# A graph layer on one core: the vector engine's transform steps placed by estimated times, row norms a stage earlier, the last transform step done pair by pair, one load moved to another queue

## The chip, the core and the metric

The kernel runs on one core of a Trainium2 chip, in fp32 throughout. A core has a matrix engine (TensorE, PE in the rows of the profile; PEld is its weight load), a vector engine (VectorE, DVE), a scalar engine (ScalarE, ACT), GpSimd (POOL) and SyncE (SP). Each engine works through its own instructions in order and waits on semaphores for the others. Transfers are issued from the instruction streams of SP, ACT or POOL, in the order of that stream, and then run on 16 DMA engines which all streams share. Matmul results land in PSUM, everything else lives in SBUF.

The metric is device time in microseconds, the median of several runs. Before the change: 2670.3 us, the median of 3 runs from 2668.56 to 2674.92.

## The reference

`x` is 64 graphs of 256 nodes with 256 features, `adj` 64 matrices of 256 x 256 zeros and ones. Cut to what matters:

```
h      = relu(layernorm(x))                       # per node
c      = relu(bn1(conv1(h)))                      # 1 tap, 256 -> 256 channels
x_conv = relu(bn2(conv2(c)) + h)                  # 17 taps along the nodes
s      = h @ w_se.T + b_se                        # 3 numbers per node
A      = exp(-dist2(s, s)) * adj
x_nmp  = A @ relu(h @ w_msg.T + b_msg)
gi, gh = [x_conv, x_nmp] @ w_ih.T, h @ w_hh.T     # three gates r, z, n of 256 each
n      = tanh(gi_n + sigmoid(gi_r + gh_r) * gh_n)
out    = x + (1 - z) * n + z * h                  # z = sigmoid(gi_z + gh_z)
```

## The kernel before

**Tiling.** Two graphs make a pair (tiles of 128 partitions x 512 columns), four pairs a block; there are 32 pairs and 8 blocks. In the code `i` is a pair, `b` a block, `j` a pair within the block. Work that needs one pair is called per pair: `norm` (layer norm: statistics on VectorE, a power on GpSimd, the scaling on VectorE), `transpose_h` (TensorE transposes, relu on ScalarE, result `hT`), `conv1`, `split`, `embed` (s), `message`, `affinity` (exp on ScalarE, then a product with `adj` on VectorE), `transpose_a`, `aggregate` (x_nmp, tile `xnm`), `gates` (called twice per pair, for the two halves of the channels) and `finish` (transposes back, adds x from tile `y`, stores).

**The convolution in transform space.** The 17-tap convolution is done for a whole block at once, as a short Fourier transform over 16 phases of the nodes, products of 16 frequency bins with the transformed filter, and a transform back. The transforms run on VectorE as lists of elementwise steps. `split` writes sums and differences of neighbouring positions into the tiles U and V. `fft.odd` (on V, temporary T, result also in Sv) gives the operands of bins 0 to 7, `fft.even` (on U, with PT and T) those of bins 8 to 15. `products(b, m)` does bins 2m and 2m+1: 24 matmul groups into three PSUM tiles, then a ScalarE copy and two VectorE instructions that read them out into Yv (m under 4) or Yu (m from 4 on; Yu is the tile V, used again). The way back is `odd_back` on Yv, `q_back` and `p_back` on Yu, `join` (four instructions that put the two halves together in V and Yv) and `residual` (adds `hT`, relu on ScalarE). The `gates` of a pair read its part of Yv.

**What sets the order.** Every engine's order is the order in which the Python code calls its instructions: nothing is rescheduled later. The transform steps are held in a queue; `pump(us)` takes steps off it until their estimated time is used up, at places chosen by hand, and `drain()` empties it. Before `gates(i, 0)` the queue is drained, all four pairs are joined and `residual` runs for all four. Inside that call, between the products that read `hT` and `xnm` and those that read Yv, the function `more` calls `conv1` of the next block's first pair.

**Buffers.** PSUM has five tiles `acc` and three tiles `aux`, taken in turn. `wb` holds three frequency bins of the filter, 768 KB each, loaded from a DRAM copy (`filt`): `products(b, m)` issues the load of bin 2m+2 ahead of its matmuls and that of bin 2m+3 behind them, each into the buffer of the bin used three before. `x` has two buffers, `adj` one, `y` one, `h1` (the result of conv1) one. SP issues the loads of `wb`, `x` and `adj`, POOL those of `y` and the stores.

A list of lines of the profile: L59, L62, L65 and L69 are the transform's steps (multiply-add, add, subtract, scaling on ScalarE), L474 to L482 `norm`, L491 `transpose_h`, L498/L500 `conv1`, L511/L512 `split`, L522 the load of a bin, L547 the products, L562/L563 their reading out, L579/L580 `residual`, L586 to L590 `embed`, L599/L602 `message`, L611 to L617 `affinity`, L627 `transpose_a`, L637 `aggregate`, L652 the products of `gates` with L658 to L682 behind them, L690 to L692 `finish`, L303 the loads of x, adj and y.

Of the kernel before, what the change touches and what calls it, by code (L numbers as in the profile page):

```python
# [38 lines left out]
class Fft:  # L39
# [27 lines left out]
    def scale(self, x, s):  # L67
        def run():
            self.a.mul(x, x, s)  # L69
            return 0  # L70
        return run
# [73 lines left out]
    def odd_back(self, Y, T):  # L145

        q = []
# [28 lines left out]
        for s in (0, 4):  # L176
            q += [self.scale(Y(0, s + 1), C8),
                  self.scale(Y(1, s), C16),
                  self.scale(Y(1, s + 1), C16 * C8),
                  self.scale(Y(0, s + 2), R2),  # L180
                  self.scale(Y(0, s + 3), R2 * C8),
                  self.scale(Y(1, s + 2), R2 * C16),
                  self.scale(Y(1, s + 3), R2 * C16 * C8)]
        return q

    def q_back(self, Y, T):

        q = [self.sub(T(0, 0, 4), Y(0, 0, 4), Y(1, 0, 4)),
# [11 lines left out]
        for s in (0, 2):  # L200
            q += [self.scale(Y(0, s + 1), R2), self.scale(Y(1, s), C8), self.scale(Y(1, s + 1), R2 * C8)]
        return q
# [28 lines left out]
def kernel(  # L231
# [155 lines left out]
    for k in range(DC):  # L387
# [9 lines left out]
        for s in fft.odd(V, T, Sv):  # L397
            s()
# [6 lines left out]
        for s in fft.even(U, PT, T):  # L405
            s()
# [49 lines left out]


    queue = deque()

    def pump(us):  # L460
        while queue and us > 0:
            us -= queue.popleft()() / 960.0 + 0.1

    def drain():
        pump(1e9)
# [4 lines left out]
    def norm(i):  # L470
        st = work.tile([P, G * MC, 6], FP, name="st")
        mv = work.tile([P, G * MC, 2], FP, name="mv")
        for j in range(G * MC):
            nc.vector.bn_stats(st[:, j, :], X[i][:, j, :])  # L474
# [170 lines left out]
    def gates(i, dc, middle=None):  # L645
# [17 lines left out]
        if middle:  # L663
            middle()
# [178 lines left out]
```

## Time and profile before

| what | value |
|---|---|
| median of 3 runs | 2670.3 us |
| the profiled execution, its own time | 2674.03 us |
| its span from first to last instruction | 2672.3 us |
| mean granted TensorE clock (1 is full) | 0.899 |
| PE busy | 2026.6 us, 76% of the span |
| DVE busy | 1485.3 us, 56% |
| ACT busy / POOL busy | 635.4 us / 127.6 us |
| DMA | 186.91 MB, mean 70 GB/s |

One profiled execution gives all rows. In a row of the timeline stand start, duration, engine, line, operation, output and inputs, the count that was merged (a fp32 matmul counts as two passes), and in brackets the idle time ahead of it and what ended it. A duration of matmuls contains a modelled end, so lengths of PE work are taken from start to start. In a row of the waits stand who waited for whom, the sum, the number and the longest. A row of the stretches gives the busy time of each engine between two times, then the granted clock, the share of the DMA engines and GB/s.

The first 217 us load and transform the filter and prepare the first block. After that the profile repeats per block, 310 to 315 us each for the first seven; the last block, which prepares no next one, takes 271 us.

### The profile page before, as it was taken

The numbers are of one execution on the slowest core, as the hardware profiler recorded it, in microseconds if no ns is written. First come the engines' busy times: TensorE is split into PE (matmuls) and PEld (weight loads), VectorE is DVE, ScalarE is ACT, GpSimd is POOL, SyncE is SP. The second block draws the span as 40 slices with busy tenths as digits, with TensorE's granted clock in tenths as the row PEclk, the third lists the DMA queues.
The fourth block names the chain that finished last, engine by engine and source line by source line (L and its number), as shares of the span: only waits on it lengthen the run. The fifth ranks groups of instructions, "written<-read, shape, count | busy, mean of one in ns | idle before, by whom it ended". The sixth has DMA issues, their size and how long they took to land.

```text
span 2672.3 us, 20737 instructions
## 1 busy us (share of the span) xinstructions
PE 2026.6 (76%) x7744; PEld 1266.3 (47%) x7744; DVE 1485.3 (56%) x2641; ACT 635.4 (24%) x1077; POOL 127.6 (5%) x191
## 2 busy tenths in 40 slices
PE   0035878886897778968788868986789777888698
PEld 0015634474445644456344744456444563447454
DVE  6846743568346663467435683367634674356822
ACT  0011322123221132113221232211321132212321
POOL 1010000000000000000000000000000000000000
PEclk9977889988999789988899879998899888998899
DMA  5433201141022401142012410214011420114101
GB/s 144 144 107 103 96 15 48 40 149 67 17 59 56 165 16 36 39 134 87 24 33 50 154 67 11 65 52 158 28 32 44 122 99 24 36 32 154 36 16 40
DMA packets 73941, 186.91 MB, mean 70 GB/s; under 512 B 15184, under 2 KB 32080, under 8 KB 73840
## 3 DMA queue, kind: packets, MB, share of 16 engines
q1 hardware_dynamic: 49152, 144.98, 16.5%
q0 software_dynamic: 18992, 33.78, 5.6%
q10 hardware_dynamic: 5696, 6.82, 0.8%
q8 instruction: 61, 1.00, 0.2%
q14 instruction: 40, 0.33, 0.0%
HBM read 156.39 MB, written 29.10 MB: 69 GB/s over the span
## 4 chain that ended last, share of the span: by engine, by line
PE 62%; DVE 19%; issue 5%; DMA 5%; ACT 4%; POOL 1%; SPq 1%; DVEq 0%; POOLq 0%; ACTq 0%
PE acc L652 33%; PE acc L547 12%; PE acc L498 5%; DMA wb<-filt 5%; PE aux L599 4%; PE aux L637 2%; PE aux L491 2%; DVE T L62 2%; DVE e L617 2%; DVE V L59 2%; DVE Yv L65 2%; PE aux L586 2%; DVE T L65 1%; ACT Yv L580 1%; DVE V L65 1%
## 5 line engine op out<-in xcount | busy, mean ns | idle before, releaser
L652 PE MATMUL acc<-hT,w_hh 128*128 128x512 f32 x768 | 350.6, 592 | 0.0
L652 PE MATMUL acc<-xnm,w_ih 128*128 128x512 f32 x768 | 350.5, 592 | 0.0
L652 PE MATMUL acc<-Yv,w_ih 128*128 128x512 f32 x768 | 342.6, 596 | 8.7 <-ACT Yv L580 8.7
L668 DVE SCALAR_TENSOR_TENSOR gn<-tr,gn 128x512 f32<-128x512 f32 x64 | 44.3, 692 | 513.2 <-ACT tr L667 513.2
L491 PE MATMUL aux<-ident,x 128*128 128x128 f32 x256 | 62.3, 392 | 244.3 <-DVE x L482 210.1
L652 PEld LDWEIGHTS acc<-Yv,w_ih 128*128 128x128 f32 x768 | 146.5, 192 | 190.3 <-issue 180.9
L498 PE MATMUL acc<-hT,w_c 128*128 128x512 f32 x256 | 162.3, 785 | 93.4 <-ACT gn L658 93.4
L652 PEld LDWEIGHTS acc<-xnm,w_ih 128*128 128x128 f32 x768 | 145.9, 190 | 183.7 <-issue 183.7
L652 PEld LDWEIGHTS acc<-hT,w_hh 128*128 128x128 f32 x768 | 144.1, 190 | 161.6 <-issue 158.4
L547 PE MATMUL acc<-U,wb 128*128 128x128 f32 x1024 | 145.0, 305 | 89.4 <-DMA wb<-filt 66.5
L547 PE MATMUL acc<-Sv,wb 128*128 128x128 f32 x512 | 84.0, 317 | 163.7 <-issue 68.9
L547 PEld LDWEIGHTS acc<-U,wb 128*128 128x128 f32 x1024 | 140.0, 219 | 95.4 <-DMA wb<-filt 68.4
L667 ACT ACTIVATE tr<-acc,b_rz 128x512 f32<-128x512 f32 x64 | 44.0, 687 | 549.9 <-PE acc L652 549.9
L491 PEld LDWEIGHTS aux<-ident,x 128*128 128x128 f32 x256 | 42.2, 187 | 264.2 <-DVE x L482 168.0
L511 DVE TENSOR_TENSOR V<-h 128x512 f32<-128x512 f32 x64 | 44.1, 689 | 217.2 <-ACT h L500 217.2
L547 PEld LDWEIGHTS acc<-Sv,wb 128*128 128x128 f32 x512 | 76.6, 227 | 172.5 <-issue 74.5
L59 DVE SCALAR_TENSOR_TENSOR V<-T,V 128x256 f32<-128x256 f32 (+2 forms) x280 | 152.7, 609 | 0.2
L547 PE MATMUL acc<-V,wb 128*128 128x128 f32 x1024 | 145.4, 303 | 0.0
L498 PEld LDWEIGHTS acc<-hT,w_c 128*128 128x128 f32 x256 | 61.8, 256 | 172.7 <-ACT gn L658 99.2
L547 PEld LDWEIGHTS acc<-V,wb 128*128 128x128 f32 x1024 | 141.4, 221 | 0.0
L599 PE MATMUL aux<-w_msg,hT 128*128 128x256 f32 x512 | 121.0, 391 | 19.8 <-ACT hT L492 19.8
L599 PEld LDWEIGHTS aux<-w_msg,hT 128*128 128x128 f32 x512 | 100.0, 197 | 52.0 <-ACT hT L492 25.9
(133 smaller groups left out, 2714.5 us busy)
## 6 DMA issues: line engine op xcount, KB each, us to landing
wb<-filt SPq DMA_DIRECT2D x120, 768.0 KB
x<-in_x_dram SPq DMA_DIRECT2D x64, 256.0 KB
adj<-in_adj_dram SPq DMA_DIRECT2D x64, 256.0 KB
y<-in_x_dram POOLq DMA_DIRECT2D x64, 256.0 KB, 5.7
out_dram<-y POOLq DMA_DIRECT2D x64, 256.0 KB, 5.2
V<-in_c_wT_dram ACTq DMA_DIRECT2D x32, 128.0 KB
filt<-V SPq DMA_DIRECT2D x8, 512.0 KB
wb<-filt SPq DMA_DIRECT2D x8, 512.0 KB
```

What stands on the lines that cost most here:

```text
L59: return self.step(out, lambda: self.v.scalar_tensor_tensor(out, x, s, y, op0=ALU.mult, op1=ALU.add))
L62: return self.step(out, lambda: self.v.tensor_add(out, x, y))
L65: return self.step(out, lambda: self.v.tensor_sub(out, x, y))
L491: nc.tensor.transpose(chunk(p, j // MC, j % MC), X[i][:, j, dc * P:(dc + 1) * P], ident)
L498: nc.tensor.matmul(p, w_c1[:, k, o * P:(o + 1) * P], HT[i][:, k, :], start=(k == 0), stop=(k == DC - 1))
L547: nc.tensor.matmul(p[kind][:, (n * DC + o) * P:(n * DC + o + 1) * P], WB[b, 2 * m + n][:, kind, k, o * P:(o + 1) * P], v[:, k::DC, 0, :], ...
L586: nc.tensor.matmul(p[:KD, :], w_se[:, k, :], HT[i][:, k, :], start=(k == 0), stop=(k == DC - 1))
L599: nc.tensor.matmul(p[:, c * D:(c + 1) * D], chunk(HT[i][:, k], g, c), w_msg[:, k, :], start=(k == 0), stop=(k == DC - 1))
L617: nc.vector.tensor_mul(e, e, ADJ[i][:, g * MC + c].rearrange("p (b h c) -> p c h b", c=MC, b=NW))
L637: nc.tensor.matmul(graph(p, g), MSG[i][:, g, c, dc * P:(dc + 1) * P], AT[i][:, g, c, :], start=(c == 0), stop=(c == MC - 1))
L652: nc.tensor.matmul(p, w[:, row:row + P], r, start=first and j == 0, stop=last and j == len(terms) - 1)
L668: nc.vector.scalar_tensor_tensor(gn, tr, 1.0, gn, op0=ALU.add, op1=ALU.mult)
```

## The change

The `pump` calls go. A class `Pace` keeps an estimate of how far TensorE and VectorE are: matmuls add their columns times 0.431/512 us per pass, VectorE instructions their elements over 960 plus 0.1 us. Ahead of a VectorE instruction that waits for another engine, `pace.vector` takes steps off the queue as long as the next one, by the estimate, ends by the time at which that input is ready; `flush(mark)` takes all steps up to a mark, where their result is needed. Other parts of the change:

- `odd` and `even` of the next block are queued behind its last `split`; what is left of `odd` is flushed ahead of `products(b, 0)`, what is left of `even` ahead of `products(b, 4)`.
- `embed` and `message` of a block's first pair come ahead of `products(b, 0)`.
- `join` is cut by pair (`part`) into four times four instructions, each four followed by that pair's `residual`; before `gates(i, 0)` reads Yv only pair 0 is flushed.
- `conv1` of the next block's first pair comes ahead of `affinity(i + 2)`, out of the middle of `gates`. `norm` of the pairs behind it is called a stage before their `transpose_h`; `x` loads are called right behind `transpose_h`.
- `adj` is loaded from POOL's stream, `y` has two buffers and is loaded two pairs ahead.
- The ScalarE scalings of `odd_back` and `q_back` become half as many instructions of twice the size, called between steps of the next part.

The core of the diff:

```diff
-        def run():
-            call()
-            return n
-        return run
+        return n, call
...
+    def odd_factors(self, Y):
+        return [self.scale(Y(c, s, 2, 4), f) for c, s, f in (
+            (0, 1, C8), (1, 0, C16), (1, 1, C16 * C8), (0, 2, R2), (0, 3, R2 * C8), (1, 2, R2 * C16),
+            (1, 3, R2 * C16 * C8))]
...
-    def join(self, Yu, Yv, T):
-        return [self.add(T(None, 0, 4), Yu(None, 4, 4), Yu(None, 0, 4)),
-                self.sub(Yu(None, 4, 4), Yu(None, 4, 4), Yu(None, 0, 4)),
-                self.sub(Yv(None, 0, 4), T(None, 0, 4), Yv(None, 0, 4)),
-                self.sub(Yv(None, 4, 4), Yu(None, 4, 4), Yv(None, 4, 4))]
+    def join(self, Yu, Yv, T, part):
+        yu, yv, t = (lambda s, v=v: v(None, s, 4).rearrange("p (o g) n e -> p o g (n e)", o=2)[:, :, part]
+                     for v in (Yu, Yv, T))
+        return [self.add(t(0), yu(4), yu(0)),
+                self.sub(yu(4), yu(4), yu(0)),
+                self.sub(yv(0), t(0), yv(0)),
+                self.sub(yv(4), yu(4), yv(4))]
+class Pace:
+    def __init__(self):
+        self.pe = self.dve = 0.0
+        self.queue = deque()
+    def tensor(self, columns):
+        self.pe += columns * 2 * 0.431 / 512
+    def run(self):
+        n, call = self.queue.popleft()
+        call()
+        if n:
+            self.dve += n / 960.0 + 0.1
+    def vector(self, n, ready=0.0):
+        while self.queue and self.dve + self.queue[0][0] / 960.0 <= ready:
+            self.run()
+        self.dve = max(self.dve, ready) + (n / 960.0 + 0.1 if n else 0.0)
+    def add(self, steps, mark=None):
+        self.queue.extend(steps)
+        if mark:
+            self.queue.append((0, mark))
+            mark.left = True
+    def flush(self, mark):
+        while mark.left:
+            self.run()
+        self.sync()
+    def sync(self):
+        self.pe = max(self.pe, self.dve + 0.2)
+class Mark:
+    left = False
+    def __call__(self):
+        self.left = False
...
-        load_rows(ADJ[i], adj, i, nc.sync)
+        load_rows(ADJ[i], adj, i, nc.gpsimd)
     def load_y(i):
-        Y[i] = work.tile([P, G * MC, D], FP, name="y")
+        Y[i] = work.tile([P, G * MC, D], FP, name="y", bufs=2)
...
+    pace = Pace()
+    def mm(p, w, v, columns, **kw):
+        nc.tensor.matmul(p, w, v, **kw)
+        pace.tensor(columns)
+    def transpose(p, v):
+        nc.tensor.transpose(p, v, ident)
+        pace.tensor(P / 2)
+    PSUM, ACT = 0.2, 0.9
...
         nc.gpsimd.tensor_tensor(rstd, rstd, neg_half, ALU.pow)
-        pump(1.2)
+        pace.vector(0, pace.dve + 1.4)
...
+        if i + 2 < B // G:
+            load_x(i + 2)
...
+        pace.vector(0, pace.pe + ACT)
...
+            pace.vector(2 * W, pace.pe + PSUM)
             nc.vector.tensor_sub(re, pv[0], pv[2])
             nc.vector.tensor_add(im, pv[0], pv[1])
...
-        if middle:
-            middle()
+        if wait:
+            wait()
         product(pr, xc, r, False, True)
         tr = work.tile([P, W], FP, name="tr")
         nc.scalar.activation(tr, pr, AF.Tanh, bias=b_rz[:, dc:dc + 1], scale=0.5)
+        pace.vector(W, pace.pe + ACT)
         nc.vector.scalar_tensor_tensor(gn, tr, 1.0, gn, op0=ALU.add, op1=ALU.mult)
-        pump(1.5)
         product(pn, xc, n, False, True)
+        pace.vector(W, pace.pe + PSUM)
...
-        if i + 1 < B // G:
-            load_y(i + 1)
-    def prepare(b, j, stats=True):
-        if b < NB:
-            i = b * PB + j
-            if stats:
-                norm(i)
-            transpose_h(i)
-            conv1(i)
-            split(j)
-            if i + 2 < B // G:
-                load_x(i + 2)
+        if i + 2 < B // G:
+            load_y(i + 2)
+    def mix(a, b):
+        q, done = [], 0
+        for j, step in enumerate(a):
+            q.append(step)
+            while done < (j + 1) * len(b) // len(a):
+                q.append(b[done])
+                done += 1
+        return q
+    odd, even, q_done = Mark(), Mark(), Mark()
+    joined = [Mark() for _ in range(PB)]
+    def forward():
+        pace.add(fft.odd(V, T, Sv), odd)
+        pace.add(fft.even(U, PT, T), even)
     load_bin(0, 0)
     load_bin(0, 1)
     load_y(0)
+    load_y(1)
     for j in range(PB):
-        prepare(0, j)
+        norm(j)
+        transpose_h(j)
+        conv1(j)
+        split(j)
+    forward()
     for b in range(NB):
         i = b * PB
-        if b == 0:
-            queue.extend(fft.odd(V, T, Sv))
-            drain()
-            queue.extend(fft.even(U, PT, T))
-        products(b, 0)
-        pump(4)
+        nxt = i + PB
         embed(i)
         message(i)
-        products(b, 1)
-        pump(5)
+        pace.flush(odd)
+        products(b, 0)
         affinity(i)
         if b > 0:
             finish(i - 1)
+        products(b, 1)
+        transpose_a(i)
         products(b, 2)
-        pump(6)
-        transpose_a(i)
+        aggregate(i)
         products(b, 3)
-        drain()
-        queue.extend(fft.odd_back(Yv, T))
-        aggregate(i)
+        pace.flush(even)
+        pace.add(fft.odd_back(Yv, T))
+        embed(i + 1)
         products(b, 4)
-        pump(6)
-        embed(i + 1)
         message(i + 1)
         products(b, 5)
-        pump(5)
+        pace.add(mix(fft.q_back(Yu, T), fft.odd_factors(Yv)))
         affinity(i + 1)
-        queue.extend(fft.q_back(Yu, T))
+        norm(nxt)
         products(b, 6)
-        pump(8)
-        if b + 1 < NB:
-            norm(i + PB)
         transpose_a(i + 1)
         products(b, 7)
-        queue.extend(fft.p_back(Yu, T))
-        queue.extend(fft.join(Yu, Yv, T))
+        pace.add(mix(fft.p_back(Yu, T), fft.q_factors(Yu)))
+        for j in range(PB):
+            pace.add(fft.join(Yu, Yv, T, slice(2 * G * j, 2 * G * (j + 1))))
+            pace.add([(W, lambda i=i, j=j, o=o: residual(i + j, o)) for o in range(DC)], joined[j])
         aggregate(i + 1)
-        pump(8)
-        if b + 1 < NB:
-            transpose_h(i + PB)
+        transpose_h(nxt)
         embed(i + 2)
         message(i + 2)
-        pump(5)
+        conv1(nxt)
         affinity(i + 2)
-        drain()
-        for j in range(PB):
-            residual(i + j)
-        def more(b=b, i=i):
-            if b + 1 < NB:
-                conv1(i + PB)
-                split(0)
-                if i + PB + 2 < B // G:
-                    load_x(i + PB + 2)
-            transpose_a(i + 2)
-        gates(i, 0, more)
+        def wait(j=0):
+            pace.flush(joined[j])
+        gates(i, 0, wait)
+        pace.flush(joined[1])
+        split(nxt)
+        norm(nxt + 1)
         gates(i, 1)
+        transpose_a(i + 2)
+        transpose_h(nxt + 1)
         aggregate(i + 2)
-        prepare(b + 1, 1)
+        conv1(nxt + 1)
+        pace.flush(joined[3])
+        split(nxt + 1)
+        norm(nxt + 2)
         gates(i + 1, 0)
         embed(i + 3)
+        transpose_h(nxt + 2)
         message(i + 3)
-        prepare(b + 1, 2)
+        conv1(nxt + 2)
+        split(nxt + 2)
         finish(i)
+        norm(nxt + 3)
         gates(i + 1, 1)
         affinity(i + 3)
         gates(i + 2, 0)
+        transpose_h(nxt + 3)
         transpose_a(i + 3)
-        prepare(b + 1, 3)
+        conv1(nxt + 3)
+        split(nxt + 3)
         if b + 1 < NB:
-            queue.extend(fft.odd(V, T, Sv))
-            even = fft.even(U, PT, T)
-            queue.extend(even)
+            forward()
         finish(i + 1)
         gates(i + 2, 1)
         aggregate(i + 3)
         gates(i + 3, 0)
         finish(i + 2)
         gates(i + 3, 1)
-        while b + 1 < NB and len(queue) > len(even):
-            queue.popleft()()
     finish(B // G - 1)```

Three places in the order of the instructions, as it stands in the two programs.

SP, one block of the stream. Before (`adj` is the load of a pair's adjacency, `wb` that of one bin):

```order
L522 DMA wb<-filt 128x1536 x4
L303 DMA adj<-in_adj_dram 128x1x512 x2
L522 DMA wb<-filt 128x1536 x8
L303 DMA adj<-in_adj_dram 128x1x512 x2
L522 DMA wb<-filt 128x1536
L522 DMA wb<-filt 128x1024
```

Now:

```order
L580 DMA wb<-filt 128x1536 x2
L343 DMA x<-in_x_dram 128x1x512 x8
L580 DMA wb<-filt 128x1536 x13
L580 DMA wb<-filt 128x1024
L580 DMA wb<-filt 128x1536 x2
```

The loads of `adj` between those of the bins have gone from this stream (they stand in POOL's), and the x loads of a block stand together.

PE, from the transposes of the next block's first x to the first products that read Yv. Before:

```order
L491 MATMUL aux<-ident,x 128x128 x8
L586 MATMUL aux<-hT,w_se 67x512 x2
L599 MATMUL aux<-w_msg,hT 128x256 x8
L611 MATMUL aux<-rd,ld 128x256 x4
L652 MATMUL acc<-hT,w_hh 128x512 x4
L652 MATMUL acc<-xnm,w_ih 128x512 x4
L652 MATMUL acc<-hT,w_hh 128x512 x2
L652 MATMUL acc<-xnm,w_ih 128x512 x2
L498 MATMUL acc<-hT,w_c_105 128x512 x4
L627 MATMUL aux<-ident,e 128x128 x8
L652 MATMUL acc<-Yv,w_ih 128x512 x6
```

Now (all matmuls of helpers bear the line of `mm`, L500, and of `transpose`, L504):

```order
L504 MATMUL aux<-ident,x 128x128 x8
L500 MATMUL aux<-hT,w_se 67x512 x2
L500 MATMUL aux<-w_msg,hT 128x256 x8
L500 MATMUL acc<-hT,w_c_105 128x512 x4
L500 MATMUL aux<-rd,ld 128x256 x4
L500 MATMUL acc<-hT,w_hh 128x512 x4
L500 MATMUL acc<-xnm,w_ih 128x512 x4
L500 MATMUL acc<-hT,w_hh 128x512 x2
L500 MATMUL acc<-xnm,w_ih 128x512 x2
L500 MATMUL acc<-Yv,w_ih 128x512 x6
```

`conv1` (w_c) has moved ahead of `affinity` (rd, ld), and `transpose_a` (ident, e) behind the gates.

DVE, from the end of `p_back` to the first instructions of `gates(i, 0)`. Before:

```order
L65 TENSOR_TENSOR V<-T,V 128x16x32
L62 TENSOR_TENSOR T<-V 128x2048
L65 TENSOR_TENSOR V<-V 128x32x64
L65 TENSOR_TENSOR Yv<-T,Yv 128x32x64
L65 TENSOR_TENSOR Yv<-V,Yv 128x32x64
L579 SCALAR_TENSOR_TENSOR Yv<-Yv,bn_scale,hT 128x512 x8
L511 TENSOR_TENSOR V<-h_398 128x8x64
L512 TENSOR_TENSOR U<-h_398 128x8x64
L511 TENSOR_TENSOR V<-h_398 128x8x64
L512 TENSOR_TENSOR U<-h_398 128x8x64
L668 SCALAR_TENSOR_TENSOR gn<-tr,gn 128x512
```

Now:

```order
L58 TENSOR_TENSOR T<-V 128x2x256
L61 TENSOR_TENSOR V<-V 128x2x4x64
L61 TENSOR_TENSOR Yv<-T,Yv 128x2x4x64
L61 TENSOR_TENSOR Yv<-V,Yv 128x2x4x64
L638 SCALAR_TENSOR_TENSOR Yv<-Yv,bn_scale,hT 128x512 x2
L58 TENSOR_TENSOR T<-V 128x2x256
L61 TENSOR_TENSOR V<-V 128x2x4x64
L61 TENSOR_TENSOR Yv<-T,Yv 128x2x4x64
L61 TENSOR_TENSOR Yv<-V,Yv 128x2x4x64
L728 SCALAR_TENSOR_TENSOR gn<-tr,gn 128x512
L731 SCALAR_TENSOR_TENSOR gn<-gn,acc 128x512
L638 SCALAR_TENSOR_TENSOR Yv<-Yv,bn_scale,hT 128x512
```

The four big instructions of `join` and the eight of `residual` are now four small and two for pair 0, then the next pair's ahead of and among the gates' own; `split` (h) follows later.

More of the change, by code (lines that the diff above doesn't have):

```diff
@@ L396 @@
         nc.vector.tensor_sub(V(0, 4), V(0, 4), e0)
-        for s in fft.odd(V, T, Sv):
-            s()
+        for _, step in fft.odd(V, T, Sv):
+            step()
         for c in range(2):
@@ L404 @@
             put(c * 4, 1, k, V(c, 0, 4)[:, 0])
-        for s in fft.even(U, PT, T):
-            s()
+        for _, step in fft.even(U, PT, T):
+            step()
         for c in range(2):
@@ L651, in product @@
             for j, (w, r) in enumerate(terms):
-                nc.tensor.matmul(p, w[:, row:row + P], r, start=first and j == 0, stop=last and j == len(terms) - 1)
+                mm(p, w[:, row:row + P], r, W, start=first and j == 0, stop=last and j == len(terms) - 1)
         r, z, n = dc * P, D + dc * P, 2 * D + dc * P
```

92 lines of the change are left out of this document (45 added, 47 removed).

## The prediction

> **What bounds the kernel now.** The page first, then the granted clock by stretches, then who waited for whom on TensorE (PE) in one whole block, then that block's timeline.
>
> ```profile
> PE 2026.6 (76%) x7744; PEld 1266.3 (47%) x7744; DVE 1485.3 (56%) x2641; ACT 635.4 (24%) x1077; POOL 127.6 (5%) x191
> 1405.00:1452.00 47.00, 47.00 (x128) 23.02 (x127) 26.78 (x38) 7.55 (x12) 3.65 (x6) 1.00 0.19 44
> 1230.00:1238.90 8.90, 0.00 (x0) 0.00 (x0) 8.90 (x24) 0.48 (x1) 0.00 (x0) 0.56 0.82 261
> ```
>
> No engine is full over the span. Where PE isn't held up (second row, between gates) it works 47.00 of 47 us at clock 1.00; where it waits (third row) the clock is 0.56 while DVE is full. So the limit is PE's own work plus waits that other engines or loads set. The block from 1151.94 to 1466.25 us (314.3 us) has these:
>
> ```profile
> PE acc L547 <- DMA wb<-filt: 17.2, 2, 9.1
> PE acc L498 <- ACT gn L658: 13.3, 1, 13.3
> PE acc L547 <- issue: 9.8, 1, 9.8
> PE aux L491 <- DVE x L482: 6.8, 2, 4.4
> PE aux L491 <- issue: 4.9, 1, 4.9
> PE acc L547 <- DVE U L62: 2.9, 1, 2.9
> PE aux L599 <- ACT hT L492: 2.8, 1, 2.8
> ```
>
> With 1.7 in four smaller ones they sum to 59.4 us ("issue" names no releaser: the 9.8 ends when DVE's last step of `odd` is done, the 4.9 when x is normalised). Behind each of the nine larger waits PE starts slowly. Two of them from the timeline:
>
> ```profile
> 1188.19 2.07 PE L547 MATMUL acc<-Sv,wb 128*128 128x128 f32 x8 [8.07 <-DMA wb<-filt]
> 1193.47 1.08 PE L547 MATMUL acc<-Sv,wb 128*128 128x128 f32 x8
> 1202.66 7.25 PE L547 MATMUL acc<-U,wb 128*128 128x128 f32 x48 [2.87 <-DVE U L62]
> 1209.75 1.88 PE L586 MATMUL aux<-hT,w_se 128*67 128x512 f32 x4
> 1211.47 3.62 PE L599 MATMUL aux<-w_msg,hT 128*128 128x256 f32 x16
> 1214.92 5.52 PE L547 MATMUL acc<-U,wb 128*128 128x128 f32 x48
> 1220.28 1.89 PE L611 MATMUL aux<-rd,ld 67*128 67x256 f32 x8
> 1222.01 1.06 PE L547 MATMUL acc<-U,wb 128*128 128x128 f32 x8
> ```
>
> Two bins take 5.36 us warm (1214.92 to 1220.28), one 2.68. Behind the wait of 8.07 one takes 5.28 (2.6 lost), behind that of 2.87 two take 7.09 (1.7 lost). Read in the same way, all nine lose 20.8 us, from 1.6 (behind the wait of 2.8) to 3.3 (behind that of 4.4), and 2.5 behind the 13.3. What remains of the block is dense: 314.3 - 59.4 - 20.8 = **234.1 us**. The change takes no matmul out, so a block can't fall below that.
>
> [...]
>
> **The change part by part.** *adj off SP.* The two waits for `wb` stand at bins 6 and 14. SP, timeline and waits:
>
> ```profile
> 1493.01 1.27 SPq L303 DMA_DIRECT2D adj<-in_adj_dram  x2
> 1494.39 38.00 SPq L522 DMA_DIRECT2D wb<-filt  x8
> 1494.39 8.24 DMA wb<-filt
> SPq L303 <- DVE e L617: 59.1, 3, 25.0
> ```
>
> The adj load waits in SP's order for DVE's last reader of the single buffer, and the bin behind it leaves SP 1.4 us after it and lands 8.24 us later. With adj on POOL a bin leaves when its buffer is free, that is when PE is done with the bin three before. Eight transposes take 0.87 us:
>
> ```profile
> 1404.46 1.04 PE L690 MATMUL aux<-ident,d 128*128 128x128 f32 x8
> 1405.33 3.60 PE L652 MATMUL acc<-hT,w_hh 128*128 128x512 f32 x8
> ```
>
> Bin 5 then has the time of bin 3, transposes and bin 4, 2.68 + 0.87 + 2.68 = 6.2 us, until PE wants it, bin 15 the same, bins 9 and 13 have 2.68 + 1.72 + 2.68 = 7.1, the others 8 or more. Bounds for what remains: nothing, or a load takes 8.1 as now, and these four come 1.9 + 1.9 + 1.0 + 1.0 us late. I take nothing, since the 8 us carried two bins, adj and two stores that left together, and they now leave spread out. Gone: the 17.2, and 2.6 + 2.8 of restarts, 22.6 us.
>
> [...]
>
> POOL gets 8 adj DMAs more per block, and what is behind them is late:
>
> ```profile
> DMA to landing us min/median/max: 4.2/5.3/9.6
> 1414.94 1.20 POOL L303 DMA_DIRECT2D y<-in_x_dram  x2 [4.82 <-DMA out_dram<-y]
> 1663.31 1.01 POOL L479 TENSOR_TENSOR rstd<-rstd,neg_half 128x4 f32<-128x4 f32 x1 [30.64 <-DVE rstd L478]
> ```
>
> The power of `norm(nxt + 3)` now stands behind finish(i)'s stores and a y load that waits for their landing: 1.2 + 5.3 + 1.2 + 1.0 = 8.7 us after y is added, against 1.9 us of DVE statistics, so DVE stands 6.8 us. Cover: PE has 12 us of `gates(i + 1, 1)` to do before DVE is wanted. I take 0; without cover 6.8 per block.
>
> *Transform ahead.* `odd` is still queued behind the last split, with three gates of PE work to go, but it now fills the idle time of DVE ahead of every gn: from 1405 to 1452 (second row above) DVE has 20.2 of 47 us free, twice the 9.8 by which it was late, and in the changed order the last step of `odd` stands ahead of the last gates' own DVE work, seven steps of `even` behind it. So the wait of 9.8 at the block's start and 2.0 behind it go, and so do 2.9 + 1.7 at products 4 (`even`). The cover is the gates' PE work, 10.3 us ahead of each gn; if it failed, 16.4 per block would stay.
>
> *norm a stage earlier, scalings spread.* The waits of PE L491 (6.8 + 4.9, restarts 2.2 + 3.3 + 2.1) and L599 (2.8 + 1.6) go: x is now normalised with a whole call of gates between it and its transposes, and the 20 scalings become 10 of twice the size, called between DVE steps, on an engine that is busy 24%. If the cover of the gates failed, 23.7 per block would stay.
>
> *What takes the place of the 13.3.* Now DVE's list from products 3 to the first pair's residual decides. Its length from the same instructions before (stretches: DVE is the third pair of numbers; then join alone, residual alone):
>
> ```profile
> 1524.29:1600.23 75.94, 51.78 (x252) 39.10 (x250) 64.93 (x110) 26.19 (x54) 1.07 (x1) 0.84 0.24 84
> 1585.78:1594.84 9.06, 2.49 (x6) 0.76 (x4) 8.99 (x5) 0.00 (x0) 0.00 (x0) 0.89 0.20 72
> 1594.84:1600.23 5.39, 0.00 (x0) 0.00 (x0) 5.39 (x8) 4.54 (x7) 0.00 (x0) 0.50 0.00 0
> 1262.10 3.60 PE L652 MATMUL acc<-hT,w_hh 128*128 128x512 f32 x8
> 1272.40 1.88 PE L498 MATMUL acc<-hT,w_c 128*128 128x512 f32 x4
> ```
>
> 64.93 - 8.99 - 5.39 = 50.55; pair 0's join is four of 512 (a quarter of 8.99, some 0.65 each with the fixed part: 2.6), its residual two of 0.67: 54.5 us. It starts 1.3 us behind products 3 (two read-outs) and waits for PE some 2.9 us (before products 5's and 7's read-outs, message, exp; between 0 and the 11.0 that DVE idles in the first row): 58.7. PE has, start to start from the rows above, embed 1.72 x 2, products 5.36 x 3 + 4.47, message 3.45 x 2, affinity 1.73 x 2, transposes 0.87 x 2, aggregate 3.45 (as message), conv1 3.43 (as eight passes of 512 in 1405.33's row), then 10.30 of gates (1262.10 to 1272.40): 53.3. So PE waits 58.7 - 53.3 = **5.4 us**, restart 2.5; with the bounds of the idle time between 2.5 and 13.5. Before, ACT's relus of all eight residuals stood ahead of the ScalarE read-out on which conv1 waited (the 13.3); conv1 now comes first, so nothing else is queued behind this wait but the products that read Yv, and behind them the gates' own chain. The DVE work of join 1 to 3 (12 x 0.65) and six residuals then stands ahead of the gn of `gates(i, 1)`, by the order: split 2.5, norm 4.4, the rest 7.3, and gn comes some 2.6 us late. ACT's tanh behind it holds up the copies of `transpose_a`, so the fourth of four transposes' PSUM tiles (three `aux`) is **2.9 us** late, restart 1.7; bounds 0 and 8.
>
> Per block: 234.1 + 5.4 + 2.5 + 2.9 + 1.7 = **246.6 us**. The ends of the blocks:
>
> ```profile
> 217.16 7.30 PE acc L547 x48
> 2401.22 7.51 PE acc L547 x48
> PE acc L547 <- DMA wb<-filt: 16.7, 2, 8.5
> PE acc L652 <- ACT Yv L580: 8.7, 1, 8.7
> ```
>
> The first products start at 217.2 (`odd`, as now). The last block (271.1 us) loses these waits, 2.9 for U, 2.3 + 1.1 small ones, 10.4 of restarts and 5.2 of embed and message, done earlier: 223.8; with 5.4 + 2.5 it is 231.7. Sum: 217.2 + 7 x 246.6 + 231.7 = 2175 us of span. The median of the runs stands 2.0 below the span shown (2670.3 to 2672.3): **2173 us**.
>
> **The rivals.** *Bins late* (chance 0.17): loads take 8.1 us, 5.8 of waits and four restarts of 1.7 per block, 8 x 12.6 = 101: 2274 us. For: the rows' 8 us. Against: no wait for bins elsewhere in the table. [...] *The fill misses* (0.06): the estimates know no slow restart, DVE idles its 11.0 in the list and the wait at the transposes grows to 8: 8 x (8.1 + 5.1) = 106, on top of late bins: 2380 us. Against: matmuls stay warm from the block's start to that list. *Slower* (0.05): the fill itself. A step put ahead of a read-out or of a gn holds up what waits for it, PSUM tiles run out, and PE stands step for step, in products and gates. DVE time of the steps per block, by line (L59, L62, L65):
>
> ```profile
> sum 314.00, DVE 41.35; mean DVE 41.35
> sum 314.00, DVE 25.59; mean DVE 25.59
> sum 314.00, DVE 25.88; mean DVE 25.88
> ```
>
> 92.8 us. All of it on PE's path gives 2173 + 8 x 92.8 = 2915 us; it is slower than now from 62 us per block, 67% of it. Against: from 1405 to 1452 steps stood between the gates' own and PE lost nothing. *No change* (0.01) needs the same to hit 62 by chance.
>
> **How the numbers follow.** The forecast, with the idle of the list up to 11.0, spans 2115 to 2240 (0.60); 0.04 lies below (no wait at Yv or aux). Range 2115 to 2295, which takes in late bins. About 0.3% is what a measurement of this kernel tells from no change. Faster: 0.60 + 0.04 + 0.17 + 0.07 + 0.06 = 0.94; same 0.01; slower 0.05.
>
> **What would show it.** Right: PE's waits for `wb`, for x and at products 0 and 4 are gone; one wait per block for Yv of 3 to 14 us, ended by ACT's relu; a clock near 0.97; blocks of some 247 us. [...]

## The result and the profile after

| what | before | after |
|---|---|---|
| median of 4 runs each | 2669.43 us | 2198.01 us (2197.2 to 2201.29) |
| ratio, with its 95% interval | | 0.8234 (0.8219 to 0.8249) |
| span of the profiled execution (its own time) | 2672.3 us (2674.03) | 2196.5 us (2198.26) |
| mean granted TensorE clock | 0.899 | 0.969 |

The change is worth 471 us. The forecast was 2173 us, 25 us (1.1%) short of the measured time, which lies within the range.

In the rows of after all matmuls stand at L500 and all transposes at L504 (they go through a helper now); L580 is the load of a bin, L343 the loads of x, adj and y, L638/L639 the residual, L649 a read-out of `embed`, L688 the copy behind `transpose_a`, L717 the copy to gn, L526/L530 power and scaling of `norm`. From the page, engine use; from the waits, those of PE in the blocks that are over 1 us (sum, number, longest):

```profile
PE 1904.0 (87%) x7744; PEld 1189.0 (54%) x7744; DVE 1497.1 (68%) x2737; ACT 623.5 (28%) x997; POOL 170.3 (8%) x255
```

```profile
PE acc L500 <- ACT Yv L639: 46.8, 8, 5.9
PE aux L504 <- ACT aT L688: 21.6, 8, 3.0
PE aux L500 <- ACT rd L649: 12.9, 7, 1.9
PE acc L500 <- DMA wb<-filt: 12.5, 7, 2.4
```

Ahead of the first products stand 161.3 us more for x and 25.2 us for Sv, and at the end 2.2 us for the last transposes. Per block remain one wait at Yv, one at the fourth PSUM tile of transposes, one at `message` and one for a bin. The waits for x (in the blocks), at products 0 and at products 4 are gone. Where the four stand, in the timeline of the block from 965.60 to 1214.33 us:

```profile
984.05 1.16 PE L500 MATMUL acc<-Sv,wb 128*128 128x128 f32 x8 [1.41 <-DMA wb<-filt]
...
1054.99 7.67 PE L500 MATMUL acc<-Yv,w_ih 128*128 128x512 f32 x12 [5.88 <-ACT Yv L639]
1062.50 3.60 PE L500 MATMUL acc<-hT,w_hh 128*128 128x512 f32 x8
...
1082.47 0.66 PE L504 MATMUL aux<-ident,x 128*128 128x128 f32 x4 [3.04 <-ACT aT L688]
1082.96 5.40 PE L500 MATMUL aux<-aT,msg 128*128 128x256 f32 x16
1088.20 3.60 PE L500 MATMUL acc<-hT,w_c 128*128 128x512 f32 x8
...
1111.69 3.72 PE L500 MATMUL aux<-w_msg,hT 128*128 128x256 f32 x16 [1.85 <-ACT rd L649]
```

The block takes 248.73 us. Waits, from the brackets: 1.41 + 5.88 + 3.04 + 1.85 = 12.18. Restarts, the time lost to slow passes behind a wait: behind Yv 7.51 us, at a granted clock of 0.70, where the same twelve passes take 5.15 warm (1129.85 to 1135.00, clock 1.00), so 2.4 (1.5 to 3.1 in the eight blocks, 2.2 in the mean); behind the 3.04 an aggregate of 5.24 instead of 3.45, so 1.8; 0.1 behind each of the other two. Dense: 232.2.

### The profile page after: what moved, and what is told of

Read it like the earlier page. It is cut to its first block, busy times and chain, and to the rows that moved or that the text cites. A ratio compares the mean times of both kernels' runs of the same rounds, so it can differ in the third digit from the quotient of the medians.

```text
span 2196.5 us, 20806 instructions
## 1 busy us (share of the span) xinstructions
PE 1904.0 (87%) x7744; PEld 1189.0 (54%) x7744; DVE 1497.1 (68%) x2737; ACT 623.5 (28%) x997; POOL 170.3 (8%) x255
## 4 chain that ended last, share of the span: by engine, by line
PE 74%; DVE 14%; DMA 3%; ACT 2%; issue 2%; POOL 1%; POOLq 0%; DVEq 0%; ACTq 0%
PE acc L500 56%; PE aux L500 15%; PE aux L504 3%; DMA wb<-filt 3%; DVE V L55 2%; DVE V L58 2%; DVE T L61 1%; DVE T L58 1%; DVE Yv L61 1%; DVE V L61 1%; DVE Yv L638 1%; DVE e L677 1%; ACT Yv L639 1%; DVE T L55 1%; POOL rstd L526 0%
## 5 line engine op out<-in xcount | busy, mean ns | idle before, releaser
L500 PE MATMUL acc<-Yv,w_ih 128*128 128x512 f32 x768 | 357.4, 617 | 46.8 <-ACT Yv L639 46.8
L500 PE MATMUL acc<-hT,w_hh 128*128 128x512 f32 x768 | 350.6, 592 | 0.0
L500 PE MATMUL acc<-xnm,w_ih 128*128 128x512 f32 x768 | 350.4, 592 | 0.0
L500 PEld LDWEIGHTS acc<-Yv,w_ih 128*128 128x128 f32 x768 | 151.6, 199 | 243.4 <-issue 185.8
L500 PEld LDWEIGHTS acc<-xnm,w_ih 128*128 128x128 f32 x768 | 145.9, 190 | 183.7 <-issue 183.7
L500 PEld LDWEIGHTS acc<-hT,w_hh 128*128 128x128 f32 x768 | 144.1, 190 | 161.6 <-issue 156.4
L504 PE MATMUL aux<-ident,x 128*128 128x128 f32 x256 | 40.3, 299 | 182.5 <-DVE x L530 161.3
L728 DVE SCALAR_TENSOR_TENSOR gn<-tr,gn 128x512 f32<-128x512 f32 x64 | 44.2, 691 | 209.3 <-ACT tr L726 209.3
L55 DVE SCALAR_TENSOR_TENSOR V<-T,V 128x256 f32<-128x256 f32 (+2 forms) x280 | 149.8, 609 | 0.5
L504 PEld LDWEIGHTS aux<-ident,x 128*128 128x128 f32 x256 | 32.0, 150 | 196.8 <-DVE x L530 163.8
L500 PE MATMUL acc<-V,wb 128*128 128x128 f32 x1024 | 128.9, 281 | 0.0
L500 PE MATMUL aux<-w_msg,hT 128*128 128x256 f32 x512 | 116.5, 380 | 12.9 <-ACT rd L649 12.9
L500 PE MATMUL aux<-aT,msg 128*128 128x256 f32 x512 | 126.0, 403 | 0.6 <-ACT aT L688 0.6
L500 PEld LDWEIGHTS acc<-V,wb 128*128 128x128 f32 x1024 | 124.0, 198 | 0.0
L500 PEld LDWEIGHTS acc<-U,wb 128*128 128x128 f32 x1024 | 120.0, 192 | 5.1 <-issue 2.5
L500 PE MATMUL acc<-U,wb 128*128 128x128 f32 x1024 | 122.1, 275 | 0.0
L500 PE MATMUL acc<-hT,w_c 128*128 128x512 f32 x256 | 119.3, 610 | 0.0
L500 PEld LDWEIGHTS aux<-w_msg,hT 128*128 128x128 f32 x512 | 96.1, 190 | 35.2 <-ACT rd L649 14.6
L500 PEld LDWEIGHTS aux<-aT,msg 128*128 128x128 f32 x512 | 102.3, 204 | 19.5 <-issue 3.8
L500 PE MATMUL acc<-Sv,wb 128*128 128x128 f32 x512 | 71.4, 285 | 37.8 <-DVE Sv L58 25.2
```

Source lines behind the costliest of these rows:

```text
L55: return self.step(out, lambda: self.v.scalar_tensor_tensor(out, x, s, y, op0=ALU.mult, op1=ALU.add))
L500: nc.tensor.matmul(p, w, v, **kw)
L504: nc.tensor.transpose(p, v, ident)
L728: nc.vector.scalar_tensor_tensor(gn, tr, 1.0, gn, op0=ALU.add, op1=ALU.mult)
```

## Experiments

All times are medians, 2198.0 is the changed kernel; the kernel before took 2668.3 to 2672.9 us in the sessions of these runs. Where a time "per block" is given, it is the mean distance between the first products of one block and those of the next, over seven blocks (248.97 us in the changed kernel: 218.84 to 1961.65).

**1. adj from POOL, alone, in the kernel before.**

```diff
-        load_rows(ADJ[i], adj, i, nc.sync)
+        load_rows(ADJ[i], adj, i, nc.gpsimd)
```

> The kernel before with one edit: the adj loads leave from POOL instead of SP. Theory (the bins were late because they stood behind adj's wait in SP's order): the two waits for wb go, 8.07 and 9.1 us with restarts of 2.6 each. DVE stood idle for PE through the whole of the first (9.55 us behind it), so it comes back in full, 10.7 per block; behind the second DVE gets back its idle 3.5 and most of the 4.6 before message, about 8 of 11.7. Sum 8 x 19 = 150 us: 2517 us, between 2488 (all of 22.6 per block) and 2585 (only the first). Rival (the issuing engine doesn't matter, the loads are slow for their own sake): 2669, with PE's waits for wb still near 9 us.

Measured: 2524.73 us, ratio to before 0.9458 (0.9442 to 0.9473), 146 us or 18.5 per block. PE's waits of this kernel:

```profile
PE aux L491 <- DVE x L482: 235.0, 25, 139.1
PE acc L547 <- DVE U L62: 32.2, 8, 4.1
```

No wait for `wb` is left; the waits for x rose by 24.9 us in all and those for U by 9.2. So the engine that issues does matter here, by the order of its stream, and the rival falls; of the 22.6 per block some 4 come back as these waits for VectorE, which is about what is missing.

**2. adj back on SP, in the changed kernel** (the same line, the other way).

> The changed kernel with one edit undone: the adj loads leave from SP again. Theory: the bins behind adj wait in SP's order for DVE's multiplication of e by adj and are late again at products 2 and 6, by some 6 us each in the changed order, with restarts of 2.5: 17.5 per block, 140 in all: 2338 us, between 2290 and 2379. Rival (the issuing engine doesn't matter): 2198 within 0.5%, and no wait for wb over 2.5 us.

Measured: 2308.88 us, 111 more. Timeline, the two waits of a block:

```profile
1031.55 2.08 PE L500 MATMUL acc<-Sv,wb 128*128 128x128 f32 x8 [5.53 <-DMA wb<-filt]
...
1076.41 2.08 PE L500 MATMUL acc<-U,wb 128*128 128x128 f32 x8 [5.07 <-DMA wb<-filt]
```

5.53 + 5.07 of waits, 1.6 + 3.0 of restarts: 15.2 in place of the 1.5 at bin 5, and 13.8 per block over all. The late bins are at products 2 and 7, not 6. The direction is the theory's; the size falls short of 17.5 because the bins are some 5.4 us late instead of 6 (85.7 us in 16 waits) and because the wait for bin 5, which the theory did not know of, goes.

**3. Norms back, right ahead of their transposes.**

```diff
         split(nxt + 1)
-        norm(nxt + 2)
         gates(i + 1, 0)
         embed(i + 3)
+        norm(nxt + 2)
         transpose_h(nxt + 2)
```

(and likewise for nxt, nxt + 1 and nxt + 3)

> The changed kernel with the four norms back right ahead of the transposes that read them (the first one product later). Theory (norms had to stand a stage earlier): behind each gates DVE has a tail of 3 us and then 4.6 us of norm, so PE waits some 6.7, 5.9 and 7.6 us at the transposes of nxt + 1 to nxt + 3, with restarts of 2 each, 26 per block; the waits of 3.0 (restart 1.8) and 1.9 us go, since PE comes later there: 19.6 net in 7 blocks, 137 in all: 2335 us (2310 to 2360). Rival (the place of the norms doesn't matter, the fill would have hidden them): 2198 to 2215.

Measured: 2316.92 us, 119 more. Timeline:

```profile
901.22 2.26 PE L504 MATMUL aux<-ident,x 128*128 128x128 f32 x8 [3.97 <-DVE x L530]
...
950.80 2.25 PE L504 MATMUL aux<-ident,x 128*128 128x128 f32 x8 [5.77 <-issue]
...
1135.09 2.21 PE L504 MATMUL aux<-ident,x 128*128 128x128 f32 x8 [5.36 <-DVE x L530]
```

Three waits of 15.1 together, where 20.2 were expected (the first 3.97 instead of 6.7), but each with a restart of 2.4 to 3.2 instead of 2: 17.5 per block in all, where 19.6 were expected. The fill doesn't hide a norm that is called late.

**4. The old fixed budgets in the new order.** `vector` lets nothing out; `pump(us)` takes steps off the queue up to a budget, at the places where it stood before.

```diff
     def vector(self, n, ready=0.0):
-        while self.queue and self.dve + self.queue[0][0] / 960.0 <= ready:
-            self.run()
-        self.dve = max(self.dve, ready) + (n / 960.0 + 0.1 if n else 0.0)
+        pass
+    def pump(self, us):
+        while self.queue and us > 0:
+            us -= self.queue[0][0] / 960.0 + 0.1
+            self.run()
```

> The changed kernel in its new order, but with the queued transform steps let out by the old fixed budgets (1.2 us in norm, 1.5, 2 and 3 in gates, 4, 5, 6, 6, 5, 8, 8 and 5 behind the products and stages) instead of by the estimated idle time of DVE. Theory (the fitting by estimates is what took away the waits at products 0 and 4): odd is late by 9.8 us again, of which embed and message (5.2), which now stand ahead of products 0, cover a part: 4.6 and a restart of 2.0; even is late by 2.9 and 1.7 again: 11 per block, 90 in all: 2288 us (2250 to 2320). Rival (the new order alone does it, the budgets were good enough): 2198 to 2210.

Measured: 2344.09 us, 146 more, 19.0 per block. PE's waits (line numbers here are two higher):

```profile
PE acc L502 <- issue: 78.0, 15, 5.8
PE aux L502 <- ACT hT L544: 42.7, 7, 6.1
PE acc L502 <- ACT Yv L641: 2.9, 1, 2.9
```

The waits at products 0 (5.8) and products 4 (4.7) are back, as the theory had it, though it put them at 4.6 and 2.9, and the time lies above its range. What it had not is the second row. ScalarE's instructions:

```profile
1095.57 1.30 ACT L64 ACTIVATE Yv<-Yv 128x512 f32<-128x512 f32 x2 [1.38 <-DVE Yv L55]
1099.29 1.15 ACT L64 ACTIVATE Yv<-Yv 128x512 f32<-128x512 f32 x2 [2.43 <-DVE Yv L61]
1100.35 1.06 ACT L544 ACTIVATE hT<-aux 128x512 f32<-128x512 f32 x2
```

The relus to hT stand in ACT's order behind scalings that wait for a transform step which VectorE has not done yet. The transposes were ready at 1093. So the scalings, too, need VectorE to be on time. But for the last block, the wait at Yv has gone; the likely reason, not tried by itself, is that PE has lost its time earlier.

**5. All residuals first, conv1 behind them.**

```diff
-        conv1(nxt)
         affinity(i + 2)
-        def wait(j=0):
-            pace.flush(joined[j])
+        pace.flush(joined[PB - 1])
+        def wait():
+            conv1(nxt)
         gates(i, 0, wait)
```

> The changed kernel with two things as before: all joins and all eight residuals ahead of gates(i, 0), and conv1(nxt) inside it, where the wait stands, instead of ahead of it. Theory (the 13.3 us of before came from ACT's relus of all residuals ahead of the read-out that conv1 needs): PE does half of conv1 and then stands until ACT's copy to gn, which comes behind the last of eight relus, 12 us behind the first: a wait of some 20 us with releaser ACT gn, and none at Yv; the products that read Yv start 17 us later, and the wait of 3.0 with its restart of 1.8 behind gates(i, 1) goes: 12.4 per block in 7 blocks, 87 in all: 2285 us (2265 to 2305). Rival (ACT's order holds nothing up, PE only needs pair 0): the wait stays at Yv and grows by conv1's 3.4: 2198 to 2225.

Measured: 2275.29 us, 77 more, 10.3 per block. PE's waits:

```profile
PE acc L500 <- ACT gn L717: 150.7, 8, 20.9
PE acc L500 <- ACT Yv L639: 5.6, 1, 5.6
```

Seven blocks wait some 21 us each for the copy to gn, behind the eight relus; the last, which has no conv1, waits 4.5 us for it and then at Yv. So this order makes such a wait, and the 13.3 us of before, with the same releaser, are read as the same. The relus in turn wait for VectorE's joins and residuals, and the run puts both back; it does not part them.

**6. The join in one piece, residuals still by pair.**

```diff
-        for j in range(PB):
-            pace.add(fft.join(Yu, Yv, T, slice(2 * G * j, 2 * G * (j + 1))))
+        pace.add(fft.join(Yu, Yv, T, slice(0, 2 * G * PB)))
+        for j in range(PB):
```

> The changed kernel with the join done for all four pairs in one go, as before, ahead of the first residual; the residuals stay by pair. Theory: the first residual comes 9.0 - 2.6 = 6.4 us later and the wait at Yv grows from 5.9 to 12.3; but 6.4 us of joins no longer stand ahead of the gn of gates(i, 1), so the wait of 3.0 and its restart of 1.8 go: net 6.4 - 4.8 x 7/8 = 2.2 per block, 18 in all: 2216 us. Rival (join by pair is worth its full 6.4 per block): 2249. Rival (it is worth nothing, the pairs' steps are done in any case before the gates need them): 2160, as the later wait goes alone.

Measured: 2228.18 us, 30 more. PE's waits:

```profile
PE acc L500 <- ACT Yv L639: 98.0, 8, 12.3
PE aux L504 <- ACT aT L688: 0.3, 1, 0.3
```

12.3 at Yv, as expected, and the wait at the transposes' tile gone. Both expected movements are there; the sum is 12 us larger, 3.5 per block instead of 2.2. Most of that stands behind `message`: the wait is as long as in the changed kernel, but in five of seven blocks the passes behind it now take 5.25 us (in the row below, from 364.72 until the next work at 369.97) instead of 3.45. The last section has more waits of equal length with and without slow passes behind them.

```profile
364.72 5.41 PE L500 MATMUL aux<-w_msg,hT 128*128 128x256 f32 x16 [1.84 <-ACT rd L649]
```

**7 to 9. Three waits, each taken away alone.** (7) Joins of pairs 2 and 3 later:

```diff
+        joins(0)
+        joins(1)
         aggregate(i + 1)
...
         gates(i, 1)
+        joins(2)
+        joins(3)
         transpose_a(i + 2)
```

(`joins(j)` is the body of the loop over pairs, which goes.) (8) Transposes ahead of `embed`, and (9) the first norm a block earlier:

```diff
-        embed(i + 3)
         transpose_h(nxt + 2)
+        embed(i + 3)
         message(i + 3)
```

```diff
         affinity(i + 1)
-        norm(nxt)
...
         finish(i + 2)
+        norm(nxt + PB)
```

> The changed kernel with the joins and residuals of pairs 2 and 3 queued behind gates(i, 1) instead of ahead of gates(i, 0). Theory (the wait of 3.0 us at the fourth transposes' PSUM tile comes from these steps, which stand ahead of the gn of gates(i, 1)): that wait and its restart of 1.8 go in 7 blocks, 34 us: 2164. DVE has 9.6 us idle behind gates(i, 1), room for the 7.5 us of steps. Rival (the steps are only moved: they now hold up split and norm of nxt + 1 and nxt + 2, and PE waits for x instead): 2198 or above. Second rival (the wait comes from ACT's four relus themselves, not from gn): the wait stays near 3 us.

> The changed kernel with transpose_h(nxt + 2) ahead of embed(i + 3) instead of between embed and message. Theory (the unforeseen wait of 1.85 us at message is for embed's PSUM tile, which ACT reads four times, because the transposes took the other two): it goes, 7 x 1.95 = 14 us: 2184. Rival (the transposes come 1.7 us sooner and now wait for the normalised x): 2198 to 2210.

> The changed kernel with norm(nxt) taken out of DVE's list between products 3 and the first residual and put behind the last finish of the block before. Theory (DVE's list decides the wait at Yv): the list is 3.7 us shorter, the wait falls from 5.9 to 2.2 and its restart from 2.4 to at most 2: 8 x 3.7 to 4.7 = 30 to 38 us: 2164. Rival (the list also waits for PE's read-outs, and DVE only idles more): 2185 to 2198.

Measured: 2172.55, 2179.58 and 2161.68 us: 25.5, 18.4 and 36.3 less than the changed kernel (ratios to before 0.8126, 0.8149 and 0.8086, each within 0.002). The rows of the waits that they aimed at, in this order; of (8) no wait for `rd` is left in the table, and the row of the transposes' tile stays as it was:

```profile
PE aux L504 <- ACT aT L688: 0.3, 1, 0.3
```

```profile
PE aux L504 <- ACT aT L688: 21.2, 7, 3.0
```

```profile
PE acc L500 <- ACT Yv L639: 26.3, 8, 5.6
PE acc L500 <- DMA wb<-filt: 3.2, 2, 1.9
```

Each theory holds, each rival falls: it was the joins ahead of gn, `embed`'s tile, and VectorE's list. The sizes differ: (7) gave 3.5 per block instead of 4.8, with more lost at bin 5 (15.7 us of waits instead of 12.5, and restarts behind five of them instead of three); (9) gave 5.8 instead of at most 4.7, because the wait for bin 5 went too, in all but two blocks. Why it went is open: products, stores and adj stand almost as before against each other, and a shift of about 1 us between them is all that the rows show.

**10 to 12. Together, and two steps further.** (10) has all three. (11) also takes the multiplication by adj for i + 2 out of the list:

```diff
-        affinity(i + 2)
+        affinity(i + 2, True)    # exp alone
...
         split(nxt)
+        weigh(i + 2)             # e times adj, then the next adj load
         norm(nxt + 1)
```

(12) has `finish(i - 1)` behind `products(b, 1)` as well.

> The changed kernel with the three edits that each took a wait away together: joins of pairs 2 and 3 behind gates(i, 1), transpose_h(nxt + 2) ahead of embed(i + 3), norm(nxt) in the block before. Theory (three separate waits, each on its own stretch of PE's path): the gains add, 25.5 + 18.4 + 36.3 = 80 us: 2118, between 2108 and 2130. Rival (they share slack: with the joins behind gates(i, 1) and the transposes earlier DVE is late for x or for the next gn): 2140 or above, with a new wait at the transposes.

> The same with the multiplication of e by adj for i + 2 (four steps, 2.1 us of DVE) taken out of the list ahead of the first residual and put behind split(nxt). Theory (what is left of the wait at Yv, 3.0 us, is still DVE's list): the wait falls to 0.9: 8 x 2.1 = 17 us less than without it: some 2101. Rival (the list is now bound by PE's last products and their read-outs): within 4 us of the run without it. Second rival (the 2.1 us come back as a late gn of gates(i, 1)): the wait at the transposes' PSUM tile returns with 2 us.

> The same again with finish(i - 1) one product later, so that 0.87 us of transposes stand between bins 3 and 4 instead of ahead of bin 2, and POOL's two stores leave after the load of bin 5 and not with it. Theory (bin 5 is late because it has the shortest time, 6.2 us, and leaves together with adj and the stores): its wait of up to 2.4 us goes where it is left: 5 to 15 us less. Rival (bin 3 or 4 is late in its place): no difference, a wait for wb one product earlier.

Measured: 2116.32, 2080.60 and 2082.69 us, ratios to before 0.7918 (0.79 to 0.7936), 0.7787 (0.7771 to 0.7804) and 0.7797 (0.7782 to 0.7811). The gains of (7) to (9) add (81.7 us of 80.2). (11) gave twice what was expected, 35.7 us. PE's waits for Yv and for bins in (10), then in (11):

```profile
PE acc L500 <- ACT Yv L639: 26.3, 8, 5.6
PE acc L500 <- DMA wb<-filt: 2.7, 2, 2.0
```

```profile
PE acc L500 <- ACT Yv L639: 3.4, 1, 3.4
PE acc L500 <- DMA wb<-filt: 2.0, 2, 1.8
```

The wait at Yv was 2.9 and went to nothing, with its restarts, though only 2.1 us of steps had left the list. VectorE's own waits in (10) show the rest: in seven blocks it stood 1.8 us for the exp ahead of those steps, which (11) does not.

```profile
DVE e L677 <- ACT e L672: 12.3, 7, 1.8
```

A block of (11) without a wait takes 231.8 us, the mean of seven is 232.2, against 237.0 in (10). In (12) the waits for bins are gone altogether, but the transposes' tile costs 0.7 per block: no gain where 5 to 15 us were expected, since there was next to nothing left to gain at bin 5. (11) is the fastest of all, 5.3% under the changed kernel.

## Why the prediction was right, and by how much it missed

The mechanism and the order of the terms held. Step by step:

- **Waits of PE plus its dense work set the time.** Held: span by span, 2196.5 us are 218.8 + 7 x 248.97 + 234.85. The forecast had 217.2 + 7 x 246.6 + 231.7. So 1.6 us come from the start, 16.6 from the seven blocks, 3.2 from the last, and 3.5 from the median, which stands 1.5 above the span here and was put 2.0 below it. That last step was a mistake: it set the median against the span of an execution that was slower than the median (2674.03 us, 1.7 above its own span).
- **Dense, 234.1.** Too high: 232.2 in the changed kernel, 231.8 in the block without waits. Since the waits of before are rows, that leaves the restarts, read too small by some 2 of 20.8 us. By luck this hides about half of the other misses.
- **5.4 at Yv, restart 2.5.** 5.88 and 2.4. VectorE's list from the end of products 3 to the first residual, busy time as the third pair of numbers:

```profile
995.64:1054.99 59.35, 53.48 (x306) 41.48 (x304) 55.94 (x107) 24.33 (x43) 3.75 (x5) 0.98 0.44 136
```

  59.35 us until PE starts again, VectorE 55.94 busy and 3.4 idle, where the sum had 58.7, with 54.5 and 4.2. What ends the wait is not quite what the sum had:

```profile
1053.37 1.42 DVE L638 SCALAR_TENSOR_TENSOR Yv<-Yv,bn_scale,hT 128x512 f32<-128x512 f32 x2
1054.22 1.33 ACT L639 ACTIVATE Yv<-Yv,bn_shift 128x512 f32<-128x512 f32 x2 [8.32 <-DVE Yv L638]
```

  PE starts at 1054.99, behind the first residual and its relu; the sum had two residuals and no relu, and these come to about the same. Some of the closeness is luck, then. Run 9 shows that it is this list which decides.
- **2.9 at the transposes' tile, restart 1.7.** 3.04 and 1.8, in six of seven blocks. Run 7 shows the cause that was given, joins ahead of gn. The forecast lists the steps that make gn 2.6 us late but not the sum, so that the number is this close is in part luck.
- **adj off SP: bins on time, taken 0 for the four tight ones.** Three of the four were on time. Bin 5 was late by up to 2.4 us, 12.5 us in seven blocks, with a restart behind three of them: the term of the sum that was mis-sized, by some 2.5 per block. The reason given for 0, that loads now leave spread out, does not hold for this bin:

```profile
976.17 1.17 POOL L343 DMA_DIRECT2D adj<-in_adj_dram  x2 [21.63 <-DVE e L677]
976.43 0.32 SPq L580 DMA_DIRECT2D wb<-filt  x1
977.32 1.21 POOL L754 DMA_DIRECT2D out_dram<-y  x2
```

  Bin 5 leaves at 976.43, between adj and two stores, and PE starts on it at 984.05: 7.6 us, where the forecast had 6.2 to spare and 8.1 as its bound. The first part, that 22.6 us per block hang on SP's order, was right in kind (run 1: 18.5; run 2: 13.8). Both agree with the row of the kernel before in which SP waits 59.1 us in a block for DVE's last reader of adj.
- **The message wait.** Not in the sum: 1.85 us per block. The step that failed is that of moving `norm` and `transpose_h`: the transposes now stand between `embed` and `message` and take two of the three `aux` tiles, so `message` needs the one that ACT reads four times for `embed` (1109.00 to 1111.63 in the block above; PE goes on at 1111.69). The order showed this; the instructions that a moved stage issues were counted, the PSUM tiles that it takes were not. Run 8 settles it.
- **POOL's power behind the stores, taken 0.** Held, with 6.6 us in six of seven blocks and 7.5 in one, where 6.8 was worked out, and no wait of PE behind it:

```profile
DVE x L530 <- POOL rstd L526: 64.8, 32, 7.5
```

- **Transform ahead, 16.4 per block; norms and scalings, 23.7.** Undone in the changed kernel, the first costs 19.0 (run 4, whose waits at products 0 and 4 are 10.5 and that behind the scalings 6.1), and the norms 17.5 (run 3). The scalings were not tried by themselves, nor were the places of `embed` and `message` ahead of products 0, the second buffer of `y` and the earlier loads of x.
- **The rivals.** Late bins came true in one bin of four. A slow fill did not: no wait of PE in the table is ended by a read-out of the products. The 0.07 in the sum of the chances was for adj's 22.6 us per block staying whichever engine issues the loads; no run shows that: run 1, which issues them from POOL, is 18.5 per block shorter, and run 2, back on SP, 13.8 longer.

Runs 2 to 5 undo 111, 119, 146 and 77 us, 453 of 471; the parts act on the same blocks, so that sum is a cross-check and no proof.

For the restart behind the wait at the transposes' tile the forecast took the row (1.6 to 1.7 behind waits of 2.8 and 2.9). The row was right here, in six of seven blocks; the last section shows the seventh beside one of the six.

## What to carry to other kernels

Where one engine runs dense, write down the work between two fixed points on each engine and count every wait from it; here that gave the two waits that were forecast within 0.5 us, if with some luck. When a stage is moved, count also the buffers it takes from a shared rotation, and what stands behind its slowest reader. A load that waits for a reader belongs in a stream where nothing urgent stands behind it (run 1: 18.5 us per block); and once waits are few, each microsecond off the longest list of the second engine can be worth more than a microsecond, since restarts can go with the waits (run 9: 3.7 us off the list, 5.8 per block; run 11: 2.1 off the list, 35.7 in all).

## What the runs showed of the hardware that was not expected

A restart is not a matter of the wait's length alone. The same wait of 3.04 us that cost 1.8 above cost 0.1 in another block, and of two waits for a bin the shorter one was followed by slow passes. Timeline of the changed kernel:

```profile
485.95 1.95 PE L500 MATMUL acc<-Sv,wb 128*128 128x128 f32 x8 [1.90 <-DMA wb<-filt]
487.69 2.83 PE L500 MATMUL acc<-V,wb 128*128 128x128 f32 x16
...
586.76 0.66 PE L504 MATMUL aux<-ident,x 128*128 128x128 f32 x4 [3.04 <-ACT aT L688]
587.25 3.72 PE L500 MATMUL aux<-aT,msg 128*128 128x256 f32 x16
...
1483.72 1.16 PE L500 MATMUL acc<-Sv,wb 128*128 128x128 f32 x8 [2.43 <-DMA wb<-filt]
1484.71 1.95 PE L500 MATMUL acc<-V,wb 128*128 128x128 f32 x16
...
1581.48 0.85 PE L504 MATMUL aux<-ident,x 128*128 128x128 f32 x4 [3.04 <-ACT aT L688]
1582.12 5.16 PE L500 MATMUL aux<-aT,msg 128*128 128x256 f32 x16
```

Sixteen passes of V took 1.95 behind the wait of 2.43 and 2.83 behind that of 1.90; the aggregate took 3.72 behind the one wait of 3.04 and 5.16 behind the other. The 5 us from the end of each of these four waits (the granted clock is the third number from the end):

```profile
485.95:490.95 5.00, 5.00 (x27) 4.95 (x28) 0.32 (x1) 0.59 (x1) 0.47 (x1) 0.66 0.76 308
586.76:591.76 5.00, 5.00 (x23) 4.03 (x24) 0.54 (x1) 2.62 (x5) 0.00 (x0) 1.00 0.29 94
1483.72:1488.72 5.00, 5.00 (x35) 4.74 (x36) 1.28 (x2) 0.88 (x2) 0.77 (x2) 1.00 0.83 312
1581.48:1586.48 5.00, 5.00 (x18) 4.18 (x19) 0.53 (x1) 2.08 (x4) 0.00 (x0) 0.66 0.27 75
```

PE was busy throughout all four; the clock was 0.66 where the passes were slow and 1.00 where they were not. Over the blocks of the changed kernel, in the same 5 us: 0.50 to 0.71 behind the eight waits at Yv (5.6 to 5.9 us each); 0.66 behind six of the seven waits of 3.0 us at the transposes' tile, 1.00 behind the seventh; 1.00 behind all seven at `message` (1.85); and of the six waits of over 1 us for a bin, 0.66 behind those of 1.90, 1.93 and 2.19, 1.00 behind those of 1.41, 1.78 and 2.43.

What sets two waits of the same length apart is open: no run here moves one of them and leaves the rest in place.
